# Routing tables built by GpSimd and VectorE rows, and the first attention chunk's steps in another order

## The chip, the cores and the metric

The kernel runs on one core of a Trainium2 chip. A core has a matrix engine (TensorE, PE in the profile), three engines for elementwise work (VectorE = DVE, ScalarE = ACT, GpSimd = POOL), a queue engine (SyncE = SP) and 16 DMA engines. Each engine takes its instructions in the order in which the program has them, and waits on semaphores for the others. The metric is the device time of one execution in microseconds (us); less is better. The program is one launch.

## The reference, cut to what matters

A small vision tower on 128 images: a tokenizer of two convolutions gives h, 128 x 64 tokens of 256 features, and two layers follow.

```python
h = _L0_tok_ref(x, ...)
h = h + _L0_attn_ref(_layernorm(h), Wq, Wk, Wv, w_mlp, b_mlp)
h = h + _L0_ffn_ref(_layernorm(h), ...)
h = h + _L1_attn_ref(_layernorm(h), ...)
h = h + _L1_ffn_ref(_layernorm(h), gate_w, gate_b, w1, b1, w2, b2)
```

Two of the parts are touched by the change. The first attention compares every query with every key of an image, in 8 groups of 32 features, through a relu and one weight vector:

```python
diff = Qg - Kg
attn = jnp.einsum('bqkgd,d->bqkg', jax.nn.relu(diff), w_mlp) + b_mlp[0]
attn = jax.nn.softmax(jax.nn.relu(attn), axis=2)
out = jnp.einsum('bqkg,bkdg->bqdg', attn, Vg)
```

The last layer sends each of the 8192 tokens to one of 8 experts, each with a capacity of 1280 tokens:

```python
probs = jax.nn.softmax(x @ gate_w + gate_b, axis=-1)
idx = jnp.argmax(probs, axis=-1)
pos = (jnp.cumsum(one_hot, axis=0) * one_hot).sum(-1).astype(jnp.int32) - 1
kept = pos < C
hmid = jax.nn.relu(jnp.einsum('ecd,edf->ecf', buf, w1) + b1[:, None, :])
ybuf = jnp.einsum('ecf,efd->ecd', hmid, w2) + b2[:, None, :]
y_tok = ybuf[idx, pos_g] * (prb * kept)[:, None]
```

## The kernel before

The stages stand one behind the other: the tokenizer; the first attention (relu_attention); the first layer's expert attention; the second layer's linear attention; the routing (route); and the experts (experts), which write the output. In the stages that the change touches the order is written out by hand: under manual_schedule each engine gets its instructions in the order of the program's text.

**The first attention** works in 8 blocks of 16 images, each in 8 chunks of 8 query positions, 64 chunks in a row. In a chunk, for each half of the features (hf), 16 image positions are worked on in three ways. VectorE does a subtract-and-relu of 128x2048 or 128x1024 elements (Chunk.relu, L639). GpSimd forms differences of 128x2048 (Chunk.difference, L655), on which ScalarE does the relu (Chunk.positive, L659). ScalarE alone does the remaining ones query by query (by_query, L671). TensorE sums all of them with the weight vector into the tile sc (Chunk.add, L486), in products of 32 columns each, four of which lie side by side in the array. The softmax of a chunk follows during the next chunk: maximum on VectorE (L688) and ScalarE (L689), less_max (L693, VectorE), exponents (L696, ScalarE), sums (L699, VectorE), weights (L703, GpSimd).

What is done before and beside a chunk hangs on names. first() prepares block 0: transposes, the statistics of rows 0 to 3 of block 1 (bn_stats and bn_aggr on VectorE, L83 and L84) and their factors (four instructions on GpSimd, L93 to L96), queries, and the first keys. first_keys and second_keys run inside chunk 0: keys(s, fo) are TensorE products in strips of 32 columns (L493), keyed(s, fo) the copy out of PSUM, by ScalarE (L537) or, with a flag, by VectorE (L535). A dictionary of further work is filled with at(n, place, ...): place "V1" of chunk n is a point in that chunk ahead of relu(0, 1), "W" comes after the previous chunk's weights, "X" after the first add.

**The routing** takes the logits of all tokens, with partition p and column t for token 64p + t, and finds each token's expert and its position in the expert's list, pos. Lists are padded to blocks of 256 rows: 39 blocks, or 78 tiles (NTILE) of 128 rows. From pos come the row in its tile (at[:, 1]) and the tile (at[:, 0]). The table pi[row, tile] = token number is made by products: for each of the 64 columns t, lh[p, r] = (r == at[p, 1, t]) is the stationary side, and hv[p, n] = (n == at[p, 0, t]) * token[p, t] the moving side, and the product is added into pi in PSUM. This goes in 8 octets of 8 columns. VectorE makes lh (L2272) and the comparison of hv (L2275) of an octet at once; ScalarE multiplies hv by the token numbers column by column (L2280); TensorE adds eight products of 128 x 128 x 78 (L2282). lh and hv have two buffers each. Then VectorE makes the two tables: rin (gather indices, L2285) directly from pi, and, through a copy id1 (L2286) and off (L2287, L2288), rout (scatter indices, L2289). Six products of a tile that nobody needs (Ctx.busy, L52) run on TensorE ahead of the table's products, another six behind them.

**The experts** then load the weights of a block (SyncE, L2340, L2341, L2344; they need only the block's expert number, which is known before the table), gather a block's rows by rin (GpSimd's queue, L2353), normalize (L2363, L2371), transpose (L2384, L2387), multiply twice (L2396, L2412) and scatter by rout (L2430). Ahead of the loop over blocks stands a prologue for blocks 0 to 2.

Of the kernel before, what the change touches and what calls it, by code (L numbers as in the profile page):

```python
# [13 lines left out]
F32 = mybir.dt.float32  # L14
# [7 lines left out]
P = 128  # L22
# [428 lines left out]
def relu_attention(c, sh, ready, wmlp, bmlp, beside):  # L451
# [10 lines left out]
    with (  # L462
# [271 lines left out]
        def first(x):  # L734

            x.xn = ready.xn
            for i in (0, 2, 1, 3):
                x.transpose(i)
                x.transposed(i, i > 1)
            for i in range(4):  # L740
                blocks[1].statistics(i)
            blocks[1].factors(0, 4)
            x.queries(0)
            x.keys(0, 0)
            x.queried(0)
            x.keyed(0, 0)
# [2 lines left out]
            x.keys(1, 0)  # L749
            x.keyed(1, 0)  # L750

        def second_keys(x, s):
            x.keys(s, 1)
            x.keyed(s, 1, s == 0)

        for b, x in enumerate(blocks):
            n = 8 * b

            if b + 1 < len(blocks):
                at(n + 9, "X", of(x.outcome, 0))  # L760
                at(n + 9, "A", of(x.outcome_copied, 0, 0))
                at(n + 9, "B", of(x.outcome_copied, 0, 1))
                at(n + 9, "Z", of(x.outcome, 1))
                at(n + 10, "O", of(x.outcome_copied, 1, 0))
                at(n + 10, "O", of(x.outcome_copied, 1, 1))
                for i in range(4):
                    at(n + 10 + i // 2, "YZ"[i % 2], of(x.back, i))
                    at(n + 10 + (i + 1) // 2, ("V2", "V1")[i % 2], of(x.added, i))
            if b == 0:
                for i in range(4):  # L770
                    at(i // 2 * 2, "XY"[i % 2], of(x.values, i))
                    at(i // 2 * 2, "AB"[i % 2], of(x.valued, i))
                continue

            if b == 1:
                at(0, "V1", *(of(x.statistics, i) for i in range(4, NP)))
                at(0, "W", of(x.factors, 4, NP))
                at(0, "C", of(x.normal, 0), of(x.normal, 1))
                at(1, "X", of(x.transpose, 0))
                at(1, "A", of(x.normal, 2), of(x.transposed, 0))  # L780
                at(1, "B", of(x.normal, 3))
                at(1, "Z", of(x.transpose, 1))
                at(2, "O", of(x.transposed, 1))
                for i in range(2):
# [50 lines left out]
        with tc.manual_schedule():  # L835
# [3 lines left out]
            for n in range(len(seq)):  # L839
# [3 lines left out]
                    first_keys(blocks[0])  # L843
                ch.difference(8, 0)
                if n == 0:
                    second_keys(blocks[0], 1)
                ch.by_query(14, 1, 0)
                ch.by_query(14, 1, 1)
                early = n > len(seq) - 5 or n % 8 == 1
# [6 lines left out]
                ch.difference(12, 0)  # L856
                ch.relu(mvp, 4, 4, 0)
                if n == 0:
                    second_keys(blocks[0], 0)
                ch.add(4, 0)  # L860
                if old:
                    old.maximum()
# [1232 lines left out]
class Routing:  # L2095


    def __init__(self, c, gp, wg, bg):
        nc = c.nc


        self.lgs = gp.tile([P, 2, 4, B], F32, name="lgs")
        self.sth = gp.tile([P, T, 4, 6], F32, name="sth")
        self.bgs = gp.tile([P, E], F32, name="bgs")
        self.wgs = gp.tile([P, 2, E], F32, name="wgs")
        self.ones = gp.tile([P, P], F32, name="ones")
        self.before = gp.tile([P, P], F32, name="before")
        self.one = gp.tile([P, T], F32, name="one")
        self.c, self.gp, self.inputs = c, gp, (wg, bg)
        self.mean, self.rs, self.largest = (gp.tile([P, T], F32, name=n) for n in ("mean", "rs", "largest"))  # L2110

    def load(self):
# [62 lines left out]
            nc.vector.scalar_tensor_tensor(y, m, 1.5, y, ALU.add, ALU.mult)  # L2175


def route(c, k, gfd, front):


# [2 lines left out]
    tc, nc = c.tc, c.nc  # L2183
    with (
        tc.tile_pool(name="mg", bufs=1) as gp,
        tc.tile_pool(name="mn", bufs=2) as np_,
        tc.tile_pool(name="mgp", bufs=1, space=PSUM) as gpp,
        tc.manual_schedule(),
    ):
# [13 lines left out]
        for x in range(2):  # L2203
            for j in range(4):
                nc.tensor.transpose(pl[:, x, j].rearrange("p s n -> p (s n)"), k.lgs[:, x, j, :], c.ident)
        for x in range(2):
            ts = slice(x * 32, x * 32 + 32)
            o = pb[:, ts, :].rearrange("p (s j n) e -> p j s n e", s=4, j=4)
# [43 lines left out]
        nc.vector.tensor_mul(cs, cs, oh)  # L2252
        nc.vector.tensor_copy(c.bexp, be)
        idle = gpp.tile([P, NBLK, E], F32, name="idle")
        c.busy(idle, past, 6)
        nc.vector.tensor_reduce(pos, cs, AX.X, ALU.add)


# [5 lines left out]
        nc.vector.tensor_single_scalar(row[:, 2], row[:, 0], P - 1, ALU.bitwise_and)  # L2264
        nc.vector.tensor_copy(at, row[:, 1:3])
        pi = gpp.tile([P, NTILE], F32, name="pi")
        NQ = 8
        for t0 in range(0, T, T // NQ):
            ts = slice(t0, t0 + T // NQ)
            lh = np_.tile([P, T // NQ, P], F32, tag="lh", name="lh")  # L2270
            hv = np_.tile([P, T // NQ, NTILE], F32, tag="hv", name="hv")
            nc.vector.tensor_tensor(  # L2272
                lh, bcast(k.lo, 1, T // NQ), bcast(at[:, 1, ts], 2, P), ALU.is_equal
            )
            nc.vector.tensor_tensor(  # L2275
                hv, bcast(k.lo[:, 0:NTILE], 1, T // NQ), bcast(at[:, 0, ts], 2, NTILE), ALU.is_equal
            )
            for i in range(T // NQ):
                t = slice(t0 + i, t0 + i + 1)
                nc.scalar.activation(hv[:, i], hv[:, i], AF.Copy, scale=k.token[:, t])  # L2280
            for i in range(T // NQ):
                nc.tensor.matmul(pi, lh[:, i], hv[:, i], start=(t0 + i == 0), stop=(t0 + i == T - 1))  # L2282
        id1 = gp.tile([P, NTILE], F32, name="id1")
        off = gp.tile([P, NTILE], F32, name="off")
        nc.vector.tensor_scalar(c.rin, pi, -1.0, 0.0, ALU.add, ALU.max)  # L2285
        nc.vector.tensor_copy(id1, pi)  # L2286
        nc.vector.tensor_scalar(off, id1, 0.0, float(2 * B * T), ALU.is_equal, ALU.mult)  # L2287
        nc.vector.tensor_add(off, off, id1)  # L2288
        nc.vector.tensor_scalar_add(c.rout, off, -1.0)  # L2289


def experts(c, hx, gfd, out, w1, w2, b2, routing):

# [8 lines left out]
    with ExitStack() as nest:  # L2302
# [138 lines left out]
        with tc.manual_schedule():  # L2441
# [7 lines left out]
            blocks[0].transpose()  # L2449
            for n in range(2):  # L2450
                blocks[n].gather((True,))
            blocks[1].moments()
            blocks[2].gather()
            blocks[1].normal()
# [19 lines left out]
def vit_tower(ctx: ExitStack, tc: tile.TileContext, a, out):  # L2474
# [21 lines left out]
    with tc.tile_pool(name="gate", bufs=1) as gp:  # L2496
        k = Routing(c, gp, a["wg"], a["bg"])
        with front.ctx:
            linear_attention(c, front, hd, hx, out, k)
            experts(c, hx, gfd, out, a["we1"], a["we2"], a["be2"], lambda: route(c, k, gfd, front))  # L2500


def layout(**i):
# [66 lines left out]
```

## Time and profile before

| What | Value |
|---|---|
| Median of three runs | 2489.36 us (2487.32 to 2489.96) |
| The profiled execution's time | 2493.15 us |
| Its span, from first to last instruction | 2491.4 us |
| First attention: first to last VectorE relu (L639) | 154.0 to 994.6 us |
| Routing: first transposed logits (L2205) to first gather (L2353) | 2021.4 to 2059.1 us |
| First expert product (L2396) | 2067.2 us |
| Mean granted TensorE clock | 0.987 |

The profile is of one execution. In lines of the timeline the columns are: start, duration, engine, source line, operation, the tile written and the tiles read, shapes, a count where several instructions are merged, and in brackets the idle time of the engine before it with the one that ended it. In lines of a group the columns are line, engine, operation, tiles, shapes and count, then the busy time in us, the mean of one in ns, and the idle time before. The table of stretches gives, for each stretch, its length and the busy time of PE, its weight loads, DVE, ACT and POOL with their numbers of instructions, the granted clock, the DMA engines' busy share and GB/s.

### The profile page before, as it was taken

How to read it: one execution, taken by the hardware profiler on the slowest of the kernel's cores; microseconds unless marked ns; L12 is line 12 of the kernel's file. 1: busy time of each engine (PE TensorE's matmuls, PEld its weight loads, DVE VectorE, ACT ScalarE, POOL GpSimd, SP SyncE). 2: the span in 40 equal slices, each digit the busy share in tenths (PEclk: the TensorE clock that was granted, in tenths of full speed). 3: DMA queues.
4: the chain of work that ended last, by engine and by line, in shares of the span. 5: the costliest groups of instructions: out<-in, count | busy, mean ns of one | idle time of the engine just before them, and what ended most of it. 6: DMA issues, size and time to landing. Idle time of an engine off the chain costs nothing. (4 is left out here: it accounts for less than half of the span.)

```text
span 2491.4 us, 88495 instructions
## 1 busy us (share of the span) xinstructions
PE 2377.8 (95%) x38897; PEld 1618.5 (65%) x38897; DVE 1997.1 (80%) x2960; ACT 1642.0 (66%) x3578; POOL 1630.3 (65%) x1283
## 2 busy tenths in 40 slices
PE   9999999999999998899999999999999879999997
PEld 5654444545445454678787877775666667888886
DVE  8789999999999999789898998886677883444443
ACT  3369999999999998667777777774554342323322
POOL 0059999999999997577887888753322305454453
PEclk9999999999999999999999999999999989999998
DMA  4100000000000000010000000002334454555554
GB/s 137 31 2 2 3 2 3 3 2 3 2 2 3 3 14 2 4 35 19 14 25 14 25 14 25 14 20 72 82 94 111 102 174 136 186 191 189 190 199 123
DMA packets 141178, 141.61 MB, mean 57 GB/s; under 512 B 108673, under 2 KB 123171, under 8 KB 132974
## 3 DMA queue, kind: packets, MB, share of 16 engines
q1 hardware_dynamic: 131932, 119.97, 16.1%
q0 software_dynamic: 7648, 14.77, 1.9%
q8 instruction: 308, 5.05, 0.8%
q10 hardware_dynamic: 1200, 1.08, 0.1%
q14 instruction: 90, 0.74, 0.1%
HBM read 103.97 MB, written 32.54 MB: 55 GB/s over the span
## 5 line engine op out<-in xcount | busy, mean ns | idle before, releaser
L655 POOL TENSOR_TENSOR m<-q,k 128x2048 f32<-128x2048 f32 x192 | 692.2, 3627 | 23.4 <-PE sc L486 22.1
L639 DVE CUSTOM_DVE_ANT_1 m<-pc,k 128x2048 f32<-128x2048 f32 (+1 forms) x320 | 652.9, 2059 | 2.2 <-ACT k L537 1.6
L486 PE MATMUL sc<-m,wide 128*32 128x512 f32 x4096 | 600.9, 600 | 23.2 <-DVE m L639 9.3
L659 ACT ACTIVATE m<-m 128x1024 f32<-128x1024 f32 x384 | 385.4, 1058 | 1.6 <-POOL m L655 1.6
L486 PEld LDWEIGHTS sc<-m,wide 128*32 128x32 f32 x4096 | 155.5, 109 | 256.3 <-issue 117.7
L671 ACT ACTIVATE m<-k,q 128x64 f32<-128x64 f32 x1024 | 264.9, 350 | 0.0
L1296 POOL TENSOR_TENSOR e<-e,mx 128x1024 f32<-128x1024 f32 x127 | 241.6, 1902 | 9.9
L1309 ACT COPY pT<-pt 128x512 f32<-128x512 f32 x256 | 133.5, 596 | 111.1 <-PE pt L1304 110.8
L2396 PE MATMUL ph<-xt,w1s 128*128 128x256 f32 x896 | 200.5, 382 | 4.5 <-ACT hT L2400 3.4
L2412 PE MATMUL po<-w2s,hT 128*128 128x256 f32 x896 | 198.0, 379 | 0.0
L2396 PEld LDWEIGHTS ph<-xt,w1s 128*128 128x128 f32 x896 | 171.0, 191 | 29.7 <-ACT hT L2400 4.6
L2412 PEld LDWEIGHTS po<-w2s,hT 128*128 128x128 f32 x896 | 168.1, 190 | 21.7
L1278 DVE TENSOR_REDUCE mx<-sc 128x16 f32<-128x1024 f32 x128 | 150.3, 1215 | 21.1 <-PE sc L1268 21.0
L2430 POOL DMA_INDIRECT out<-y,rout x56 | 56.6, 1010 | 168.3 <-ACT hT L2400 129.3
L1288 DVE TENSOR_REDUCE mx<-e 128x16 f32<-128x1024 f32 x128 | 154.7, 1209 | 7.8 <-ACT e L1285 6.1
L2417 ACT ACTIVATE y<-y,gf 128x256 f32<-128x256 f32 x56 | 28.0, 507 | 197.4 <-issue 112.9
L2400 ACT ACTIVATE hT<-ph,w1s 128x256 f32<-128x256 f32 x224 | 93.0, 470 | 98.5 <-PE ph L2396 81.5
L1285 ACT ACTIVATE e<-e 128x1024 f32<-128x1024 f32 x128 | 133.8, 1061 | 33.8 <-DVE e L1282 30.5
L1282 DVE TENSOR_TENSOR e<-sc,mx 128x1024 f32<-128x1024 f32 x128 | 150.1, 1213 | 0.1
L1193 ACT COPY kr<-pqk 128x512 f32<-128x512 f32 x248 | 127.3, 601 | 24.4 <-PE pqk L1186 24.4
L1304 PE MATMUL pt<-ident,e 128*128 128x128 f32 x1024 | 130.2, 277 | 11.0 <-POOL e L1296 9.4
L1319 PEld LDWEIGHTS pz<-pT,vr 128*64 128x64 f32 x4096 | 125.4, 138 | 21.4 <-ACT pT L1309 11.1
(360 smaller groups left out, 4745.2 us busy)
## 6 DMA issues: line engine op xcount, KB each, us to landing
w1s<-in_we SPq DMA_DIRECT2D x30, 1028.0 KB
w2s<-in_we SPq DMA_DIRECT2D x30, 1024.0 KB
h<-hd SPq DMA_DIRECT2D x4, 2048.0 KB
hx<-h SPq DMA_DIRECT2D x4, 2048.0 KB
out<-h SPq DMA_DIRECT2D x4, 2048.0 KB
hd<-h SPq DMA_DIRECT2D x15, 512.0 KB
x<-hd SPq DMA_DIRECT2D x12, 512.0 KB
xt<-in_x SPq DMA_DIRECT2D x16, 256.0 KB
```

What stands on the lines that cost most here:

```text
L486: nc.tensor.matmul(dst[j : j + 32], wide[:, hf, s : s + 32], part, start=start, stop=stop)
L639: nc.vector._custom_dve(TENSOR_ADD_SAT, out=m, in0=bcast(self.pc[:, o : o + n * 8].rearrange("p (t i) -> p t i", i=n), 3, T), in1=bcast(se ...
L655: nc.gpsimd.tensor_tensor(m, bcast(self.q[:, hf, s : s + 4], 3, T), k, ALU.add)
L659: nc.scalar.activation(m, m, AF.Relu)
L671: nc.scalar.activation(self.parts[i, hf][:, q], self.blk.k[:, hf, i], AF.Relu, bias=self.q[:, hf, i - NB // 2, q : q + 1],)
L1278: nc.vector.tensor_reduce(mx, self.sc[x].rearrange("p h c s -> p (h c) s"), AX.X, ALU.max)
L1282: nc.vector.tensor_sub(e, self.sc[x].rearrange("p h c s -> p (h c) s"), bcast(self.sm[x], 2, T))
L1285: nc.scalar.activation(self.e[x], self.e[x], AF.Exp, scale=SCALE)
L1288: nc.vector.tensor_reduce(self.sm[x], self.e[x], AX.X, ALU.add)
L1296: eng.tensor_mul(e, e, bcast(sm, 2, T))
L2396: nc.tensor.matmul(ph[:, j], self.w1[:, w0 : w0 + P], self.xt[:, fc], start=(fc == 0), stop=(fc == 1))
L2412: nc.tensor.matmul(po, self.hT[:, f, r * P : r * P + P], self.w2[:, f, :], start=(f == 0), stop=(f == 7))
```

## The change

In the first attention: three of the four statistics of block 1's second half move from chunk 0's place "V1" into first(), behind the factors of the first half; the factors of the second half move from chunk 0 to chunk 1. TensorE's product keys(0, 1) moves up behind keys(1, 1), ahead of the first add; VectorE's copy of it stays where it was.

In the routing: hv is no longer made by one comparison on VectorE and eight multiplications on ScalarE per octet. Each of its rows is one instruction with two operations (compare with the tile number, multiply by the token number); six rows of an octet are GpSimd's, two (i = 3 and 7) VectorE's, each with tiles of their own. Each product is cut into four strips of 32 columns. The pool of lh and hv has three buffers in place of two. lh compares with a copy of lo in PSUM, which VectorE makes after the transposes of the logits. The products of the unneeded tile go from six to four. rout is made later, in the experts' prologue, by results().

```diff
@@ first(x)
             blocks[1].factors(0, 4)
+            for i in range(4, 7):
+                blocks[1].statistics(i)
             x.queries(0)
@@
-        def second_keys(x, s):
-            x.keys(s, 1)
-            x.keyed(s, 1, s == 0)
+        def second_keys(x):
+            x.keys(1, 1)
+            x.keyed(1, 1)
+            x.keys(0, 1)
@@
-                at(0, "V1", *(of(x.statistics, i) for i in range(4, NP)))
-                at(0, "W", of(x.factors, 4, NP))
+                at(0, "V1", of(x.statistics, 7))
+                at(1, "W", of(x.factors, 4, NP))
@@ chunk 0, behind ch.difference(8, 0)
-                    second_keys(blocks[0], 1)
+                    second_keys(blocks[0])
@@ chunk 0, behind ch.relu(mvp, 4, 4, 0)
-                    second_keys(blocks[0], 0)
+                    blocks[0].keyed(0, 1, True)
@@ class Routing
+        self.id, self.off = (gp.tile([P, NTILE], F32, name=n) for n in ("id", "off"))
...
+    def results(self):
+        nc, off = self.c.nc, self.off
+        nc.vector.tensor_scalar(off, self.id, 0.0, float(2 * B * T), ALU.is_equal, ALU.mult)
+        nc.vector.tensor_add(off, off, self.id)
+        nc.vector.tensor_scalar_add(self.c.rout, off, -1.0)
@@ route
-        tc.tile_pool(name="mn", bufs=2) as np_,
+        tc.tile_pool(name="mn", bufs=3) as np_,
...
+        lo = gpp.tile([P, P], F32, name="lo")
+        nc.vector.tensor_copy(lo, k.lo)
...
-        c.busy(idle, past, 6)
+        c.busy(idle, past, 4)
...
-        NQ = 8
+        NQ, hi = 8, k.lo[:, 0:NTILE]
         for t0 in range(0, T, T // NQ):
             ts = slice(t0, t0 + T // NQ)
             lh = np_.tile([P, T // NQ, P], F32, tag="lh", name="lh")
-            hv = np_.tile([P, T // NQ, NTILE], F32, tag="hv", name="hv")
             nc.vector.tensor_tensor(
-                lh, bcast(k.lo, 1, T // NQ), bcast(at[:, 1, ts], 2, P), ALU.is_equal
+                lh, bcast(lo, 1, T // NQ), bcast(at[:, 1, ts], 2, P), ALU.is_equal
             )
-            nc.vector.tensor_tensor(
-                hv, bcast(k.lo[:, 0:NTILE], 1, T // NQ), bcast(at[:, 0, ts], 2, NTILE), ALU.is_equal
-            )
+            hv = {}
             for i in range(T // NQ):
+                eng, name = (nc.vector, "v") if i % 4 == 3 else (nc.gpsimd, "g")
+                if i in (0, 3):
+                    hv[name] = np_.tile([P, T // NQ, NTILE], F32, tag=f"hv{name}", name="hv")
                 t = slice(t0 + i, t0 + i + 1)
-                nc.scalar.activation(hv[:, i], hv[:, i], AF.Copy, scale=k.token[:, t])
+                eng.tensor_scalar(hv[name][:, i], hi, at[:, 0, t], k.token[:, t], ALU.is_equal, ALU.mult)
             for i in range(T // NQ):
-                nc.tensor.matmul(pi, lh[:, i], hv[:, i], start=(t0 + i == 0), stop=(t0 + i == T - 1))
+                v = hv["v" if i % 4 == 3 else "g"][:, i]
+                for j in range(0, P, 32):
+                    nc.tensor.matmul(
+                        pi[j : j + 32], lh[:, i, j : j + 32], v, start=(t0 + i == 0), stop=(t0 + i == T - 1)
+                    )
         nc.vector.tensor_scalar(c.rin, pi, -1.0, 0.0, ALU.add, ALU.max)
-        nc.vector.tensor_copy(id1, pi)
...
+        nc.vector.tensor_copy(k.id, pi)
@@ experts, prologue
             for n in range(2):
                 blocks[n].gather((True,))
+            results()
             blocks[1].moments()
```

More of the change, by code (lines that the diff above doesn't have):

```diff
@@ L2270, in route, with experts @@
             lh = np_.tile([P, T // NQ, P], F32, tag="lh", name="lh")
-            hv = np_.tile([P, T // NQ, NTILE], F32, tag="hv", name="hv")
             nc.vector.tensor_tensor(
-                lh, bcast(k.lo, 1, T // NQ), bcast(at[:, 1, ts], 2, P), ALU.is_equal
+                lh, bcast(lo, 1, T // NQ), bcast(at[:, 1, ts], 2, P), ALU.is_equal
             )
-            nc.vector.tensor_tensor(
-                hv, bcast(k.lo[:, 0:NTILE], 1, T // NQ), bcast(at[:, 0, ts], 2, NTILE), ALU.is_equal
-            )
+            hv = {}
             for i in range(T // NQ):
+                eng, name = (nc.vector, "v") if i % 4 == 3 else (nc.gpsimd, "g")
+                if i in (0, 3):
+                    hv[name] = np_.tile([P, T // NQ, NTILE], F32, tag=f"hv{name}", name="hv")
                 t = slice(t0 + i, t0 + i + 1)
-                nc.scalar.activation(hv[:, i], hv[:, i], AF.Copy, scale=k.token[:, t])
+                eng.tensor_scalar(hv[name][:, i], hi, at[:, 0, t], k.token[:, t], ALU.is_equal, ALU.mult)
             for i in range(T // NQ):
[L2282 to L2285, printed above, removed]
-        nc.vector.tensor_copy(id1, pi)
[L2287 to L2292, printed above, removed]
+                v = hv["v" if i % 4 == 3 else "g"][:, i]
[3 more added lines that the diff above has]
+                    )
+        nc.vector.tensor_scalar(c.rin, pi, -1.0, 0.0, ALU.add, ALU.max)
+        nc.vector.tensor_copy(k.id, pi)
+def experts(c, hx, gfd, out, w1, w2, b2, routing, results):
     tc, nc = c.tc, c.nc
@@ L2499, in vit_tower @@
             linear_attention(c, front, hd, hx, out, k)
-            experts(c, hx, gfd, out, a["we1"], a["we2"], a["be2"], lambda: route(c, k, gfd, front))
+            experts(c, hx, gfd, out, a["we1"], a["we2"], a["be2"], lambda: route(c, k, gfd, front), k.results)
 def layout(**i):
```

## The prediction

> **What bounds the kernel now.** I read the page first, then the timeline of the two stages that the change touches, then the groups of GpSimd's instructions.
>
> ```profile
> span 2491.4 us, 88495 instructions
> PE 2377.8 (95%) x38897; PEld 1618.5 (65%) x38897; DVE 1997.1 (80%) x2960; ACT 1642.0 (66%) x3578; POOL 1630.3 (65%) x1283
> ```
>
> The stages run one behind the other, so a microsecond gained inside one is gained at the end if the work behind it starts earlier. The share of busy PE says little: what ends last must be read in each stage. In the first attention it is VectorE (DVE): in the stretch 250 to 280 us it is busy 29.83 of 30, and the largest wait of ScalarE (ACT) from 152 to 230 us, 4.3 us in three times, is for it. At the start of that stage VectorE itself idles twice:
>
> ```profile
> 152.26 0.18 DVE L84 BATCH_NORM_AGGREGATE mv<-st 128x2 f32<-128x6 f32 x1
> 154.01 2.29 DVE L639 CUSTOM_DVE_ANT_1 m<-pc,k 128x2048 f32<-128x2048 f32 x1 [1.56 <-ACT k L537]
> 156.22 0.14 DVE L480 TENSOR_SCALAR least<-bm 128x1 f32<-128x1 f32 x1
> 156.28 2.28 DVE L639 CUSTOM_DVE_ANT_1 m<-pc,k 128x2048 f32<-128x2048 f32 x1
> 161.12 0.69 DVE L535 TENSOR_SCALAR k<-pk 128x512 f32<-128x512 f32 x1 [2.56 <-PE pk L493]
> 161.72 1.21 DVE L639 CUSTOM_DVE_ANT_1 m<-pc,k 128x1024 f32<-128x1024 f32 x1
> 162.86 0.42 DVE L83 BATCH_NORM_STATS2 st<-h 128x6 f32<-128x256 f32 x1
> ...
> 164.99 2.26 DVE L639 CUSTOM_DVE_ANT_1 m<-pc,k 128x2048 f32<-128x2048 f32 x1
> ```
>
> The reader sees 1.56 us of waiting for the first keys and 2.56 us for the second, and four statistics between 162.86 and 164.99.
>
> In the routing, a single chain of dependent work runs with everything else stopped; the experts start on its end:
>
> ```profile
> 2036.81 0.23 DVE L2265 CAST at<-row 128x128 f32<-128x128 int32 x1
> 2053.28 4.12 ACT L2280 ACTIVATE hv<-hv,token 128x78 f32<-128x78 f32 x16 [0.57 <-PE pi L2282]
> 2053.70 4.21 PE L2282 MATMUL pi<-hv,lh 128*128 128x78 f32 x32 [0.48 <-ACT hv L2280]
> 2057.94 0.24 DVE L2285 TENSOR_SCALAR rin<-pi 128x78 int32<-128x78 f32 x1 [2.74 <-PE pi L2282]
> 2058.87 0.20 DVE L2289 TENSOR_SCALAR rout<-off 128x78 int32<-128x78 f32 x1
> 2059.07 1.26 POOL L2353 DMA_INDIRECT g<-hx,rin  x1 [69.61 <-DVE rout L2289]
> 2062.26 0.43 DVE L2363 BATCH_NORM_STATS2 st<-g 128x6 f32<-128x256 f32 x1 [3.19 <-DMA g<-hx,rin]
> ```
>
> ACT scales 16 rows (two octets) in 4.12 us, waits 0.57 for PE, and repeats: from `at` ready (2037.04) to `rin` (2057.94) go 20.9 us. What replaces ACT is GpSimd (POOL), and the price of its instruction decides:
>
> ```profile
> L1067 POOL TENSOR_SCALAR row<-h,mv,rs 128x256 f32<-128x256 f32 x20 | 24.6, 1231 | 0.2 <-issue 0.2
> L107 POOL TENSOR_SCALAR xn<-h,rs,nb 128x256 f32<-128x256 f32 x24 | 13.4, 557 | 0.0
> L1666 POOL TENSOR_SCALAR rs<-mv 128x4 f32<-128x4 f32 x15 | 3.4, 229 | 146.4 <-DVE mv L1661 131.3 <-ACT vT L1739 15.1
> L2144 POOL TENSOR_SCALAR_AFFINE_SELECT before<-before 128x128 f32<-128x128 f32 x1 | 0.3, 292 | 0.1
> ```
>
> The same form, two operations with two per-row scalars on 128x256, takes 557 ns as multiply-add (L107) and 1231 ns as subtract-multiply (L1067).
>
> **The change, part 1: first chunk.** Three statistics (pitch 0.53 us: 150.22 to 150.77) go into the first gap: 152.44 + 1.60 = 154.04, against 154.01; cost 0.03. The keys that VectorE copies are now the fourth of PE's row of key products; three take 5.36 from 151.40, so a fourth (1.71) ends at 158.5, just as VectorE comes free at 158.56: the 2.56 gap shrinks to about 0.1. VectorE reaches the relu of 164.99 at 160.9, 4.1 us early. What is late next? The maximum of the first chunk (VectorE, 173.89 before) needs its last sum, which needs ACT's relu of GpSimd's third difference. GpSimd runs its three differences from 155.78 to 166.57 as before, and ACT is without a gap from 163.02 to 172.9 (that relu 168.00 to 170.00). PE's sum of 1.07 follows, so the maximum starts at 171.1: 2.8 us of the 4.1 are left. ACT takes it at 172.9, its 1.72 us wait before 174.62 gone; VectorE's next step, 175.63 before, needs that result and starts at 173.2: 2.4 us are left. Behind it VectorE had no gap until 215 (0.47 us), while ACT had two more (2.01 and 0.57), so 2.4 carries on. The four factor instructions on GpSimd (1.9 us) move to the next chunk, whose wait for VectorE (1.65 before 193.66) covers them; without it they would delay the next difference by 1.9. Moving the product ahead of PE's first sum delays that sum by 1.7 us; nothing waits for it but a buffer needed at 163.4. Value **-2.4**; bounds -4.1 (all of VectorE's idle) and 0 (ACT takes over at once); a loss is excluded by VectorE's unchanged work.
>
> **Part 2: the rows.** Removed: 8 comparisons of 800 ns on VectorE and 64 ACT scalings. Added: 48 rows on GpSimd and 16 on VectorE. VectorE per octet: lh 1.14 (pitch) plus two rows of 0.20 (the 128x78 TENSOR_SCALAR of L2287, 201 ns), 1.54; eight make 12.3 us. PE per octet: eight rows of four strips; six rows of 128 columns take 1.09 us less 0.22 of latency (161.71), 0.145 a row, at most 1.2 us, and at a granted clock of 0.50, as in 2034 to 2037, 2.4. GpSimd per octet: six times X.
>
> X has no row. Interpolated to 78 columns from 229 ns at 4, the multiply-add gives 229 + 328 x 74/252 = 0.325, and subtract-multiply 229 + 1002 x 74/252 = 0.52. The one comparison on GpSimd that the trace has, the affine select, does 128 columns in 292 ns; that can't be had at the slow pace (0.72 at 128). Scaled from a 128x5 iota of 140 ns it is 0.23 at 78. I take the row nearest in operation, a comparison, but with a scalar form's fixed cost: between 0.23 and 0.325, X = 0.31. Ends 0.23 and 0.62 (subtract-multiply with the 0.10 us gap seen between L1067 and L1075 at 1046.31). GpSimd starts 0.15 after `at` (as L2366 does after L2364): 2037.19 + 48 x 0.31 + 0.54 (before: last scaling to `rin`) = 2052.6, so `rin` is **5.3 earlier**. PE stays under it unless its clock stays at 0.50.
>
> The Trainium skill speaks against this part: "GPSIMD Engine Reference", section "Engine selection", gives elementwise work to VectorE and calls GpSimd about twice as slow for two-input operations. Twice VectorE's 0.20 would be 0.40 a row, 19.2 us in all and `rin` at 2056.9, 1.0 earlier; the rows here say 1.4 times (557 against VectorE's 404, both L107) or 3 times, by the pair of operations, so I keep the rows. "SBUF — State Buffer", section "Who interferes with whom", says a VectorE instruction in a 2-port mode and GpSimd lock each other out; VectorE's form with two scalars from memory (L2371, 410 ns for 256) is too slow for such a mode, so I add nothing, and if it locked, 16 rows waiting 0.31 each would add 5.0 to VectorE's 12.3 and put `rin` at 2055.0.
>
> **Part 3: collision.** The six expert weight loads are issued from 2036.69 on, and hold the DMA engines to 2056 whatever the tables do:
>
> ```profile
> 2050.00:2056.00 6.00, 5.52 (x45) 5.37 (x44) 4.39 (x5) 5.43 (x22) 0.00 (x0) 1.00 0.95 391
> 2056.00:2059.00 3.00, 2.48 (x18) 2.12 (x17) 0.96 (x5) 1.40 (x6) 0.00 (x0) 1.00 0.03 12
> ```
>
> (Last columns: granted clock, DMA share, GB/s.) Before, the gather came after them and landed in 3.19 us. Now it is issued at 2053.8, among them. A later gather with a weight load in flight (2077.86 to the statistics at 2082.10) took 4.24: **+1.05**. Bounds 0 and +2.2, the rest of the loads.
>
> **Part 4, at nothing.** The copy of `lo` lies in VectorE's 0.81 us wait before 2023.24; without it, 0.2. Two idle products fewer free PE at 2038.0, before the first rows. The outgoing table: the trace names `rout` as what the gather waited for, but scatters start 0.82 us after their input ends (2107.67 to 2108.49) and the gather 0.89 after `rin` ended, so it waited for `rin`; value 0, bound -0.75 (if it waited for the last VectorE instruction). Its three instructions (0.7 us) now stand behind the transpose's copy and delay the second block's statistics, which end at 2068.25 while GpSimd, issuing gathers, takes them at 2070.37; without that cover, 0.7.
>
> **Sum:** -2.4 - 5.3 + 1.05 = -6.65. The profiled run is 2493.15 us with a span of 2491.4; it goes to 2486.5. The median shown is 2489.36, 3.8 under it, and goes to 2482.7.
>
> **Rivals.** (a) GpSimd compares at the slow pace, X = 0.52: rows end at 2062.15, `rin` at 2062.7, +4.8; the loads are over, no collision; with -2.4 it is +2.4, 2491.8. For: L1067 and its 1229 ns kin are the majority of such rows. Against: the affine select. (b) Slower: the same place at a dearer price, GpSimd being the bound of the octet. At X = 0.62, 29.8 us, `rin` at 2067.5, +9.5, with -2.4 it is +7.1, 2496.5. It decides against the change from X = 0.47 and by over 0.2% from 0.574. For: nothing here shows a comparison with a multiply. (c) The first chunk gives nothing because ACT, gap-free from 203 to 292, sets the pace: -5.3 + 1.05 = -4.25, 2485.1. Against: ACT's three gaps of 4.3 us before 203. (d) VectorE bounds the octets (X under 0.25): `rin` at 2037.08 + 12.3 + 0.6 = 2050.0, -7.9 + 1.05 - 2.4 = -9.3, 2480.1.
>
> **Chances.** About 0.2%, 5.0 us, is what can be told from no change here. Forecast 0.42, (d) 0.18, (c) 0.06, (a) 0.2, (b) 0.14. Faster by over 0.2%: the forecast and (d), 0.60; within: (a) and (c), 0.26; slower: 0.14. The range runs from X = 0.23 with all 4.1 us of the first gap (-11, 2478.4) to just past (a), 2493, leaving (b) out; the likeliest case's own is 2478.4 to 2486.
>
> **What would show it.** GpSimd rows of 0.23 to 0.33 us, 48 of them, ACT without the scalings, VectorE waiting for nothing before 161 us, its maximum near 171, `rin` about 15.5 us behind `at`, the first gather landing in over 4 us. It is wrong if GpSimd's rows take over 0.47, if VectorE's rows stretch beside them, if PE's clock stays at 0.50 through the octets, or if the chunk at 300 us is no earlier than before.

## The result, and the profile after the change

The changed kernel takes 2501.12 us, the median of five runs (2499.84 to 2505.07), beside 2488.76 (2487.24 to 2489.96) for the kernel before on the same chip: a ratio of 1.0054, 95% interval [1.0039, 1.0069]. It is slower, by about half a per cent. The profiled execution took 2499.84 us with a span of 2498.0 (before: 2491.4). That is 1.3 under its median, where the one of before was 4.4 over its own, so the two traces show 6.6 of the 12.4 us.

| Start of | before, us | after, us | difference |
|---|---|---|---|
| maximum of the first chunk (L688) | 173.9 | 171.6 | -2.3 |
| last VectorE relu of the first attention (L639) | 994.6 | 991.8 | -2.8 |
| indices `at` of the table | 2036.81 | 2036.69 | -0.1 |
| `rin` | 2057.94 | 2067.86 | +9.9 |
| first gather | 2059.07 | 2068.40 | +9.3 |
| first expert product | 2067.23 | 2076.60 | +9.4 |
| last scatter | 2479.4 | 2486.0 | +6.6 |

Below the table the difference shrinks by 2.8 us; 1.6 of it lie in the first expert products, which took 8.75 us for 32 records in before's execution, at a granted clock of 0.82, and 7.17 in this one, at 1.00.

Three things stand in the trace. First, the first attention, in VectorE's timeline of the changed kernel:

```profile
158.94 0.69 DVE L535 TENSOR_SCALAR k<-pk 128x512 f32<-128x512 f32 x1
161.23 8.95 DVE L639 CUSTOM_DVE_ANT_1 m<-pc,k 128x2048 f32<-128x2048 f32 x4
171.58 0.69 DVE L688 TENSOR_REDUCE mx<-sc 128x8 f32<-128x512 f32 x1 [1.40 <-PE sc L486]
```

The copy of the second keys waits for nothing (2.56 us before), the relu that stood at 164.99 starts at 161.23, and the maximum waits 1.40 us for TensorE's sum. Second, the time won there is gone before the table begins. VectorE's timeline from the row statistics (`mean`) to the logits, in the kernel before:

```profile
2014.21 0.88 DVE L2155 TENSOR_REDUCE mean<-sth 128x64 f32<-128x512 f32 x1
2023.24 1.14 DVE L2211 TENSOR_TENSOR x<-pl,rs 128x64 f32<-128x64 f32 x8 [0.81 <-PE pl L2205]
```

and after the change:

```profile
2010.42 0.86 DVE L2159 TENSOR_REDUCE mean<-sth 128x64 f32<-128x512 f32 x1
2016.68 0.29 DVE L2218 COPY lo<-lo 128x128 f32<-128x128 f32 x1 [3.11 <-ACT hT L1892]
2016.88 0.68 DVE L2165 TENSOR_REDUCE x<-x 128x64 f32<-128x512 f32 x1
2023.12 1.14 DVE L2224 TENSOR_TENSOR x<-pl,rs 128x64 f32<-128x64 f32 x8 [1.21 <-PE pl L2216]
```

VectorE stands for 3.11 us ahead of the new copy of `lo`, until ScalarE has read out the part of PSUM that the copy goes to (so the trace's releaser); the sums and the logits queue behind it. The stretch takes 12.70 us in place of 9.03. In all five kernels of this document in which VectorE makes this copy it takes 12.2 to 12.7, in the twelve others 9.0 to 9.1. Third, the table itself, in the timeline of all engines and in the table of stretches (columns as before: granted clock, DMA share and GB/s last):

```profile
2036.69 0.23 DVE L2278 CAST at<-row 128x128 f32<-128x128 int32 x1
2037.17 29.82 POOL L2293 TENSOR_SCALAR hv<-lo,at,token 128x78 f32<-128x78 f32 x48 [50.87 <-DVE at L2278]
2053.07 1.22 DVE L2284 TENSOR_TENSOR lh<-lo,at 128x1024 f32<-128x1024 f32 x1 [2.01 <-PE pi L2297]
2054.21 0.55 DVE L2293 TENSOR_SCALAR hv<-lo,at,token 128x78 f32<-128x78 f32 x2
2067.86 0.24 DVE L2300 TENSOR_SCALAR rin<-pi 128x78 int32<-128x78 f32 x1 [9.41 <-PE pi L2297]
2068.40 1.27 POOL L2365 DMA_INDIRECT g<-hx,rin  x1 [1.41 <-DVE id L2301]
```

```profile
2044.00:2050.00 6.00, 5.10 (x108) 2.79 (x104) 2.31 (x4) 0.00 (x0) 6.00 (x11) 0.50 0.93 366
2056.00:2062.00 6.00, 5.23 (x112) 3.00 (x112) 1.68 (x3) 0.00 (x0) 6.00 (x10) 0.50 0.11 41
```

GpSimd's 48 rows take 29.82 us without a gap, 0.62 each; VectorE waits 2.0 us in each of the last four octets, so it has room. From `at` to `rin` go 31.17 us in place of 21.13. And TensorE's granted clock is 0.50 from 2040.9 to 2071.7, after 3.4 us at 1.00; in the kernel before it was 1.00 from 2039.7 to 2067.0.

### The profile page after: what moved, and what is told of

It is laid out like the page before. It is cut to its first block, busy times and chain, and to the rows that moved or that the text cites. A ratio compares the mean times of both kernels' runs of the same rounds, so it can differ in the third digit from the quotient of the medians.

```text
span 2498.0 us, 89249 instructions
## 1 busy us (share of the span) xinstructions
PE 2375.6 (95%) x39277; PEld 1611.6 (65%) x39277; DVE 1995.4 (80%) x2969; ACT 1626.0 (65%) x3514; POOL 1661.5 (67%) x1331
## 5 line engine op out<-in xcount | busy, mean ns | idle before, releaser
L639 DVE CUSTOM_DVE_ANT_1 m<-pc,k 128x2048 f32<-128x2048 f32 (+1 forms) x320 | 653.0, 2059 | 0.3 <-PE sc L486 0.3
L1196 ACT COPY kr<-pqk 128x512 f32<-128x512 f32 x248 | 127.3, 600 | 24.3 <-PE pqk L1189 24.3
L1322 PEld LDWEIGHTS pz<-pT,vr 128*64 128x64 f32 x4096 | 124.7, 138 | 21.1 <-ACT pT L1312 11.1
```

Of the source, the lines that this page charges most:

```text
L639: nc.vector._custom_dve(TENSOR_ADD_SAT, out=m, in0=bcast(self.pc[:, o : o + n * 8].rearrange("p (t i) -> p t i", i=n), 3, T), in1=bcast(se ...
```

## The experiments

All of them compute the whole result. The measure of the table is the time from the start of `at` to the start of `rin`, in the profiled execution of each.

| Kernel | `at` to `rin`, us | idle products ahead | products | rows made by |
|---|---|---|---|---|
| before | 21.1 | 6 | whole | ScalarE |
| attn_only, attn_late | 21.0 each | 6 | whole | ScalarE |
| after | 31.2 | 4 | strips | 6 GpSimd, 2 VectorE |
| after6 | 31.1 | 6 | strips | 6 GpSimd, 2 VectorE |
| lo_act | 31.3 | 4 | strips | 6 GpSimd, 2 VectorE |
| lo_sbuf | 37.9 | 4 | strips | 6 GpSimd, 2 VectorE |
| g3 | 23.1 | 4 | strips | 3 GpSimd, 5 VectorE |
| rows_before | 24.3 | 4 | strips | ScalarE |
| no_strips | 30.3 | 4 | whole | ScalarE |
| busy4_only | 29.1 | 4 | whole | ScalarE |
| best | 30.0 | 4 | whole | 4 ScalarE, 4 GpSimd |
| best6 | 17.3 | 6 | whole | 4 ScalarE, 4 GpSimd |
| best8 | 18.6 | 8 | whole | 4 ScalarE, 4 GpSimd |
| strips6 | 24.8 | 6 | strips | 4 ScalarE, 4 GpSimd |
| act3 | 18.9 | 6 | whole | ScalarE, three buffers |

**The first chunk alone** (attn_only: the kernel before with the edits of the first attention, the first five hunks of the diff).

> The kernel before with the first attention's part of the change alone. If the first chunk's new order is worth what the changed kernel's trace shows up to the routing (3.8 us early at the row sums of the routing), the time falls by 2.5 to 4 us, ratio 0.9985 to 0.999, the first maximum at about 171.5 us and the last relu of VectorE near 991.8. The rival, that the gain is spent on the way whatever the routing does (in the changed kernel the routing's indices were ready at 2036.7, against 2036.8 before): ratio 1.000, indices ready at 2036.8.

Measured over five rounds: ratio 0.9988 [0.9973, 1.0003]. In the trace the first maximum is 2.4 us earlier and the last relu 2.1. Over all the traces the last relu starts at 994.0 to 995.0 in the three kernels without the new order and at 990.9 to 992.7 in the fourteen with it, so the gain inside the first attention is shown. That it reaches the table is not: `at` is 2.1 earlier here and `rin` 2.3, but the start of the row statistics scatters from 2007.1 to 2016.7 over the seventeen executions, and prices and busy4_only, which have the old first chunk, have `at` at 2034.7 and 2032.3. The interval of the ratio holds 1.

**GpSimd's prices** (the kernel before with 24 instructions more on GpSimd, three of a kind, into tiles that nobody reads).

> The kernel before with 24 more instructions of GpSimd on tiles that nobody needs, in the linear attention. Theory: every pair of operations but multiply-add runs at one slow pace with a larger fixed part, so compare-multiply and subtract-multiply both take 0.62 us at 78 columns and compare-multiply 0.79 at 128 (0.62 + 50 x 3.42 ns), multiply-add 0.3. Rival: the comparison itself is dear: compare-multiply 0.62, subtract-multiply 0.5 or less, and a comparison alone over 0.4. A product of two tensors of four rows (312 columns) 0.7 to 0.8, by the 1.85 ns a column of the weights' product.

The groups of these instructions (the scalars `one` and `token` are read from memory, one for each partition):

```profile
L2157 POOL TENSOR_SCALAR d<-lo,one,token 128x128 f32<-128x128 f32 x3 | 2.4, 795 | 0.3
L2170 POOL TENSOR_TENSOR w<-lo,token 128x312 f32<-128x312 f32 x3 | 2.1, 705 | 0.2
L2161 POOL TENSOR_SCALAR d<-lo,one,token 128x78 f32<-128x78 f32 x3 | 1.9, 647 | 0.3
L2155 POOL TENSOR_SCALAR d<-lo,one,token 128x78 f32<-128x78 f32 x3 | 1.9, 644 | 4.7 <-DVE one L2147 4.5
L2165 POOL TENSOR_SCALAR d<-lo,token 128x78 f32<-128x78 f32 x3 | 1.5, 488 | 0.3
L2163 POOL TENSOR_SCALAR d<-lo,one 128x78 f32<-128x78 f32 x3 | 1.4, 478 | 0.3
L2159 POOL TENSOR_SCALAR d<-lo,one,token 128x78 f32<-128x78 f32 x3 | 1.2, 413 | 0.3
```

L2155 and L2157 are the table's own form, compare and multiply, at 78 and 128 columns: 644 and 795 ns. Subtract and multiply (L2161) costs the same 647, multiply and add (L2159) 413, a comparison alone (L2163) 478, a product alone (L2165) 488. So the comparison is not dear in itself: of the three pairs tried, both that are not multiply-add cost the same. With the rows of 256 columns (1231 and 557 ns), and subtract-multiply taken for the slow pair, that pair is (1231 - 644) / 178 = 3.3 ns a column on a fixed 387, multiply-add 0.8 on 350. Four rows by one plain multiplication (L2170) cost 705, little more than one row of the pair.

**The rows** (rows_before: the changed kernel with VectorE's one comparison and ScalarE's scalings; g3: three rows of an octet on GpSimd and five on VectorE; no_strips: rows_before with whole products).

```diff
-                eng, name = (nc.vector, "v") if i % 4 == 3 else (nc.gpsimd, "g")
+                eng, name = (nc.vector, "v") if i % 3 else (nc.gpsimd, "g")
```

> The changed kernel with the rows of hv made as before (one comparison on VectorE and eight scalings on ScalarE per octet), all else kept: strips, three buffers, lo in PSUM, outgoing table late. If GpSimd's 48 rows of 0.62 us are the loss, the time from the indices to rin goes from 31.2 us to 8 x 2.06 + 1.9 + 0.5 = 18.9, ratio about 0.9995. The rival, that strips, buffers or TensorE's clock hold the octets: it stays over 25 us, ratio over 1.002.

> The changed kernel with three rows of an octet on GpSimd (i = 0, 3, 6) and five on VectorE, in place of six and two. If GpSimd's price a row sets the octet (0.62), it falls from 3.7 us to what VectorE needs, 1.14 + 5 x 0.25 = 2.4: 19.2 us and 0.8 of tail, 20 us from the indices to rin in place of 31.2. Rival: the strips' instructions arrive late as soon as GpSimd is no longer the slower: 24 us or more, with gaps on TensorE that nothing explains.

> The rows made as before and each product whole (128 columns) again; three buffers and lo in PSUM stay. In the run with the rows as before, TensorE stood 3.07 and 2.10 us with nothing that the profile shows to wait for, while the DMA engines were 96% busy with weights. Theory: the strips' fourfold number of instructions arrives late while the weights load; then whole products have no such gaps, and from the indices to rin it takes 18.9 us in place of 24.3. Rival: TensorE's granted clock (0.50 to 0.70 in that run) is the loss, whatever the products' form: still over 22 us.

rows_before came to a ratio of 1.0006 [0.999, 1.0021], so the rows hold most of the loss; g3 took 2494.07 and no_strips 2500.11, one run each. Taking GpSimd's price away gives 7 to 8 of the 10 us back, but not the rest, and with whole products nothing at all: there is a second bound under the first. In no_strips TensorE was busy without a gap at a granted clock of 0.50, 27.6 us for the 64 products (128 records). That points to the four idle products.

**The idle products** (busy4_only: the kernel before with the one edit below; after6: the changed kernel with the reverse).

```diff
-        c.busy(idle, past, 6)
+        c.busy(idle, past, 4)
```

> The kernel before with four idle products in place of six ahead of the table's products, and nothing else. Theory (the two idle products keep TensorE's clock up): the granted clock stays at 0.50 in 2044 to 2060 us where it was 1.00, the 64 whole products take about 0.43 us each (27.5 us in all), and from the indices to rin go 29 to 30 us in place of 21; the whole kernel 6 to 8 us longer (ratio about 1.003). Rival (the clock's state in those kernels came from something else, the longer row work for instance): the clock is 1.00 again, indices to rin 21 us, time the same.

> The changed kernel with six idle products again in place of four. Theory: the clock returns to 0.8 or 1.0 during the octets, but GpSimd's 48 rows of 0.62 us set the pace, so rin still comes 30.5 to 31.5 us after the indices; only what follows rin (the first expert product) may gain up to 1 us; ratio to the kernel before 1.004 to 1.006. Rival (TensorE's slow clock is a second cause of the loss beside GpSimd's rows): indices to rin 25 us or less, ratio 1.002 or less.

busy4_only: ratio 1.0032 [1.0022, 1.0042], about 8 us from two products left out that nobody reads. TensorE's timeline and one of its stretches:

```profile
2029.25 4.34 PE L52 MATMUL idle<-past,ident 128*128 128x312 f32 x8 [2.35 <-issue]
2034.96 26.36 PE L2282 MATMUL pi<-hv,lh 128*128 128x78 f32 x128 [1.38 <-ACT hv L2280]
```

```profile
2040.00:2046.00 6.00, 6.00 (x30) 6.00 (x29) 3.65 (x4) 3.72 (x15) 0.00 (x0) 0.50 1.00 385
```

and the same of best6, which has six idle products:

```profile
2026.67 5.45 PE L52 MATMUL idle<-past,ident 128*128 128x312 f32 x12 [2.34 <-issue]
2032.08 14.90 PE L2297 MATMUL pi<-hv,lh 128*128 128x78 f32 x128
```

```profile
2040.00:2046.00 6.00, 6.00 (x54) 6.00 (x54) 4.85 (x6) 3.34 (x12) 2.12 (x3) 1.00 1.02 419
```

TensorE is busy 6.00 of 6 us in both. At clock 1.00 it gets 54 records done, at 0.50 30. Four idle products do lift the clock in busy4_only: it is 1.00 from 2033.3, just as they end, to 2036.7. TensorE then waits 1.38 us for the first product, the clock falls back, and 24.6 us of gapless products do not lift it again. In the seven kernels with whole products and six or eight idle ones the clock rises and stays at 1.00 to the end of the table; in the ten others, with four idle products or with strips, it does not. Of these ten, best and no_strips never have it above 0.50 in the table. Nor do four always cost the time: of best's twelve executions, 2483.49 to 2506.32 us, the fastest has a mean clock of 0.992 and the slowest 0.979. After6 stayed at a ratio of 1.0038 [1.0024, 1.0051] and 31.1 us: there GpSimd's rows hold the octets whatever the clock does, and the clock, 0.98 in 2038 to 2044, falls to 0.50 again. The products come in short bursts there, 8 to 24 records at a time; that the bursts let it fall was not tested.

**The copy of `lo`** (lo_sbuf: no copy, lh reads `lo` from SBUF; lo_act: ScalarE makes the copy).

```diff
-        nc.vector.tensor_copy(lo, k.lo)
+        nc.scalar.copy(lo, k.lo)
```

> The changed kernel without the copy of lo into PSUM; VectorE's comparison reads lo from SBUF. If the copy's wait for its PSUM bank (3.11 us before 2016.68 in the changed kernel) is a loss on the chain, the indices are ready 3.2 us earlier, near 2033.5, and the time is 3 us under the changed kernel's, ratio about 1.004. The rival, that VectorE's comparison with both inputs in SBUF and GpSimd's rows hold each other up: rows of GpSimd from 29.8 us to as much as 39.6 (eight comparisons of 1.22), ratio 1.005 to 1.008.

> The changed kernel with the copy of lo into PSUM made by ScalarE, which has nothing else to do there. If the copy's place in VectorE's order was the loss, the indices come 3.1 us earlier than in the changed kernel (about 2033.5) and GpSimd's 48 rows stay at 29.8 us, as lo is still in PSUM: rin near 2064.7. Rival: the wait for the bank is a wait for something on the chain: indices at 2036.7 as before.

In lo_sbuf the wait of 3.11 us is gone, the stretch from `mean` to the logits takes 9.03 us again, and `at` is 3.7 us earlier than in the changed kernel; but the same 48 rows take longer:

```profile
L2291 POOL TENSOR_SCALAR hv<-lo,at,token 128x78 f32<-128x78 f32 x48 | 36.5, 774 | 47.8 <-DVE at L2276 47.8
```

36.53 us in place of 29.82, ratio 1.0055 [1.0034, 1.0075]. So the copy is there for a reason: each of the eight lh comparisons with both inputs in SBUF (1.22 us) holds GpSimd up by 6.7 / 8 = 0.84 us. Row by row, eight rows take 1.44 to 1.61 us to the start of the next, one beside each comparison, and the 39 others 0.61 to 0.62. In lo_act (2500.52, one run) ScalarE's copy holds nothing up: the stretch takes 9.03 us and the rows 29.89. Its `at` is at 2036.85 all the same, because that execution reached the row statistics 3.8 us later than the changed kernel's (2014.24 against 2010.42).

**Putting it together** (best: first chunk, copy on ScalarE, VectorE's comparison of hv at once, four rows of an octet scaled by ScalarE and four by one GpSimd multiplication, whole products, three buffers, outgoing table later; best6, best8: six and eight idle products in place of four; strips6: best6 with strips; attn_late: the kernel before with the first chunk and the later outgoing table; act3: attn_late with three buffers).

```diff
+            for i in range(4):
+                t = slice(t0 + i, t0 + i + 1)
+                nc.scalar.activation(hv[:, i], hv[:, i], AF.Copy, scale=k.token[:, t])
+            nc.gpsimd.tensor_mul(hv[:, 4:8], hv[:, 4:8], bcast(k.token[:, t0 + 4 : t0 + 8], 2, NTILE))
```

> What the runs point to: the first attention's part kept; lo copied into PSUM by ScalarE; hv compared on VectorE at once, its first four rows scaled on ScalarE and its last four on GpSimd in one product of two tensors (0.70 us); whole products; three buffers. VectorE then needs 1.86 us an octet: 14.9 us and 1.0 of tail, 16 us from the indices to rin in place of 21.1 before; if TensorE's whole products (0.23 to 0.26 each) are the bound, 17.5. With the first attention's 2 to 3 us: 6 to 8 us under the kernel before, ratio 0.997 to 0.9975. Rival: GpSimd's product and VectorE's comparisons hold each other up, over 20 us and ratio 0.999 or more.

> The combined kernel (first chunk laid anew, ScalarE's copy of lo, comparison of hv on VectorE at once, four rows of an octet scaled by ScalarE and four by one GpSimd multiplication, whole products, three buffers, outgoing table later) with six idle products in place of four. Theory: the clock returns to 1.00, indices to rin 16 to 19 us in place of 30, the first gather 2 to 5 us earlier than before besides the 2 us of the first chunk, ratio 0.997 to 0.9985. Rival (the clock stays at 0.50 because the products follow each other too loosely): indices to rin about 30 us and a ratio of 1.003 again.

> The combined kernel with eight idle products in place of six. Theory (with six the clock comes up too late in some executions, which takes the gain away): the clock is 1.00 through the octets, indices to rin 17 to 18 us, the executions spread less upwards and the ratio is 0.997 to 0.999. Rival (the spread has another source, the linear attention's clock): median and ratio as with six products, 0.999 to 1.000.

> The combined kernel with six idle products and the table's products in strips of 32 columns, as in the changed kernel. Theory (the strips bring waits of their own, since TensorE's instructions, four times as many, come late while the weights load): gaps of 1 to 3 us ended by issue in the table's products, indices to rin 20 to 23 us in place of the 17.3 with whole products, ratio 1.001 to 1.002. Rival (the gaps came with the slow clock): no such gaps, indices to rin 15 to 17 us, ratio as with whole products or better.

> The kernel before with the first chunk laid anew and the outgoing table made later, the rest of the routing as before. Theory (both parts are worth their own): the first gather starts about 0.55 us after rin starts in place of 1.13, so 0.5 to 0.6 us more than with the first chunk alone: 2.6 us under the kernel before at the first gather, ratio 0.9985 to 0.9993. Rival (the wait for rout cost nothing): the gather still starts 1.1 us after rin, ratio that of the first chunk alone or nearer to 1.

> The kernel before with the first chunk laid anew, the outgoing table made later and three buffers for lh and hv in place of two; ScalarE scales all rows, GpSimd does nothing in the table. Theory (the late first scatter belongs to the GpSimd multiplication; with three buffers ScalarE, 2.11 us an octet, is the table's bound): indices to rin 18 to 19 us in place of 21, the clock 1.00, the first gather 1.1 us after rin, the first scatter 1.65 us after its tile's last addition starts, TensorE's wait for the third block under 2 us, ratio 0.997 to 0.9985. Rival (the scatter is late for another reason, the earlier gather among the weight loads for instance): the first scatter 3.7 us after the addition here too, or the table still 21 us, ratio 0.999 to 1.000.

| Kernel | median, us | before beside it, us | ratio, 95% interval |
|---|---|---|---|
| best | 2501.09 | 2489.94 | 1.0033 [1.0015, 1.0052] |
| best6 | 2487.59 | 2489.89 | 0.9999 [0.9984, 1.0013] |
| best8 | 2487.80 | 2490.05 | 0.9994 [0.9983, 1.0004] |
| strips6 | 2494.72 | 2490.05 | 1.0013 [1.0002, 1.0024] |
| attn_late | 2488.08 | 2489.89 | 0.9994 [0.9981, 1.0008] |
| act3 | 2488.76 | 2492.20 | 0.9985 [0.9971, 0.9999] |

best and best6 differ in two idle products: 30.0 against 17.3 us. strips6 differs from best6 in the strips, and its TensorE timeline shows what they cost:

```profile
2040.27 0.91 PE L2298 MATMUL pi<-hv,lh 128*32 128x78 f32 x41 [0.55 <-ACT hv L2293]
2043.60 2.38 PE L2298 MATMUL pi<-hv,lh 128*32 128x78 f32 x127 [2.42 <-issue]
2049.82 4.38 PE L2298 MATMUL pi<-hv,lh 128*32 128x78 f32 x127 [3.84 <-issue]
2055.89 3.15 PE L2298 MATMUL pi<-hv,lh 128*32 128x78 f32 x89 [1.68 <-issue]
```

Three times TensorE waits for nothing but its own next instruction, 7.9 us in all, after the first 169 of the 512 records and twice after 127 more; the clock falls to 0.50 in 2050 to 2056. The DMA engines, which load the expert weights, are 73 and 101% busy in the first two gaps, but 4% in the third. rows_before and g3 show such gaps too, the whole products none. The even spacing, 127 products and as many weight loads, suggests that instructions reach TensorE in portions and come late; that is not shown, and neither is a share of the weight loads in it.

best6's table is 3.8 us shorter than before's, but its end is not earlier than act3's by the times. In all four kernels with the GpSimd multiplication, and in no other, the first scatter starts 3.72 to 3.75 us after its tile's last addition in place of 1.65; gathers queue behind it, and TensorE's third block waits 4.6 to 4.9 us in place of 1.8 at most. From best6:

```profile
2077.16 0.69 DVE L2437 TENSOR_TENSOR y<-y,g 128x512 f32<-128x512 f32 x1
2080.91 1.08 POOL L2440 DMA_INDIRECT out<-y,rout  x1 [8.46 <-PE po L2422]
2094.42 2.07 PE L2406 MATMUL ph<-xt,w1s 128*128 128x256 f32 x4 [4.63 <-ACT hT L2410]
```

and from act3, where GpSimd does nothing in the table:

```profile
2085.63 0.69 DVE L2432 TENSOR_TENSOR y<-y,g 128x512 f32<-128x512 f32 x1
2087.28 1.08 POOL L2435 DMA_INDIRECT out<-y,rout  x1 [6.36 <-PE pt L2389]
2100.81 1.99 PE L2401 MATMUL ph<-xt,w1s 128*128 128x256 f32 x8 [1.50 <-ACT hT L2405]
```

The late scatter goes with the GpSimd multiplication, and only the first of 28 blocks has it; what it waits for stays open. The four kernels are also the only ones with exactly eight more instructions in GpSimd's stream, and no run tells the two apart. act3 is the one kernel whose interval lies below 1, by little: its table is 2.2 us shorter, bounded by ScalarE now (64 scalings in 16.13 us without a gap), and the first chunk's 2 us may be in it. Among eleven such intervals, one that just clears 1 is weak evidence.

## Why the prediction was wrong, point by point

**The rows, the failed step.** "I take the row nearest in operation, a comparison, but with a scalar form's fixed cost: between 0.23 and 0.325, X = 0.31." The rows take 0.62, twice that: GpSimd's 48 rows end at 2067.0, and `rin`, expected at 2052.6, comes at 2067.86, 15.3 us of the 18.4 between the forecast median (2482.7) and the measured one. Two errors lie in the price. The affine select compares with a pattern and has no scalars from memory, so its 292 ns priced another instruction; a comparison with a scalar from memory costs 478 at 78 columns. And the interpolations began at a 229 ns row of 4 columns with one operation and a constant, where the forms with scalars from memory have a fixed part of 350 to 390 ns. The upper end, 0.62, was met by luck: it was 0.52 for the instruction and 0.10 for a gap, and the rows have no gap and cost 0.61 to 0.65 by themselves. Rival (b), with a chance of 0.14, had the mechanism, GpSimd as the bound of the octet, and the place: `rin` 9.5 us later (measured 9.9). That the profiled execution also came out at its total, 7.1 us more (measured 6.7), is luck again: it counted 2.4 us of gain that had gone before `at`, and the first expert products behind the table happened to be 1.6 us faster. The median, 2501.12, is 4.6 above its 2496.5.

The Trainium skill, "GPSIMD Engine Reference", section "Engine selection", calls GpSimd about two times slower than VectorE for elementwise work with two inputs. A row here has one tensor and two scalars as inputs, so the sentence is not quite about it. The prediction set it aside for rows that said 1.4 or 3 times and took 0.31 beside VectorE's 0.20. Measured side by side it was 0.62 to 0.27 us a row, 2.3 times.

**The idle products, priced at nothing.** "Two idle products fewer free PE at 2038.0, before the first rows." They do, and the clock is 0.50 in the table from 2040.9 on. In the changed kernel this costs nothing that can be told, as after6 shows, because GpSimd is slower still; without GpSimd's rows it costs 8 us (busy4_only). The text had the sign to look for, "if PE's clock stays at 0.50 through the octets", but no price for it.

**The copy of `lo`, priced at nothing.** "The copy of `lo` lies in VectorE's 0.81 us wait before 2023.24." It is ordered 6.6 us earlier and waits 3.11 us for its place in PSUM; lo_sbuf, without it, has `at` 3.7 us earlier than the changed kernel, and both executions reached the row statistics at 2010.4. The price is larger than the first chunk's gain.

**The strips**, at most 1.2 us an octet at full clock: the products themselves fit that, but not the gaps that end by issue, 7.9 us in strips6. The changed kernel, which GpSimd paces, shows none of them.

**The first chunk, -2.4:** right inside the first attention, -2.3 at the first maximum and -2.1 to -2.8 at the last relu; that it carries on to the end is not shown. The wait of the maximum for the sum (1.40 us) is the one it named.

**The outgoing table, 0:** right. In attn_late the gather starts 1.14 us after `rin` starts, as in before (1.13), though the trace names a different releaser. Where the changed kernel shows 0.54, it is GpSimd that differs: idle for 1.4 to 9.1 us ahead of the gather (nine kernels) it starts 0.54 to 0.55 after `rin`, idle for 68 to 82 us (the other eight, before among them) 1.13 to 1.14. Which of these kernels' differences does it was not tested.

**The collision, +1.05:** not tried by the changed kernel, whose gather came after the weight loads. In best6 the gather was issued at 2047.56 with the DMA engines full until about 2048 and landed in 3.22 us, against 3.19. That is nothing, but an overlap of 0.4 us is not the 2.2 that the forecast had; such a collision no run tried.

**The rule about shared access.** The prediction weighed only the part of "SBUF — State Buffer", section "Who interferes with whom", on the fast modes, and added nothing. The same section says that a VectorE instruction with two inputs in SBUF holds up a GpSimd instruction that reads there. lo_sbuf shows that part: 0.84 us of GpSimd for each comparison. It explains why the change copies `lo` to PSUM.

## What to carry to other kernels

Price an instruction of GpSimd only from a row of the same pair of operations with the same kind of scalars, and when the bounds are a factor of 2.7 apart and the chain is 48 long, take the dear end as a full case. Work that only keeps TensorE busy is part of the timing: ask what the clock will be in the stage behind it before calling its removal free. When one bound is removed and the time hardly moves, look for the next one at the same height: here GpSimd's rows, the slow clock and the strips' gaps each held the table at 23 to 31 us.

## What the hardware showed unexpectedly

- TensorE's clock can stay down under gapless work: 24.6 us of gapless table products at 0.50 in busy4_only, 14.90 us of the same products at 1.00 in best6. In the eight kernels with six idle products the clock rises 2.9 to 6.0 us after the first of them starts (attn_only 2.9, best6 4.1, attn_late 4.3, before 6.0). Four take 3.7 to 4.5 us; with them it rises after 2.9 to 4.1 us in five kernels, falling back 3.4 to 13.7 us later, and in the other three not before the table's products begin. The Trainium skill, "TensorE: Matmul & The Clock Gate", section "What's actually happening", has the clock rise after about 3.4 us of sustained work, at a point that varies from run to run. The idle products agree with it, the 24.6 us do not. The idle products move 312 columns for each load of 128, the table's 78; that this share decides was not tested.
- A GpSimd indirect transfer starts 0.6 us later behind 70 us of idleness than behind 9 us or less, in all seventeen kernels; whether the idleness does it was not tested.
- Short products can starve: 512 strip records brought gaps of 1.2 to 3.8 us ended by issue in strips6, rows_before and g3, 128 whole ones none. In the four kernels in which six GpSimd rows pace the octet, the strips show none.
